# A second gathered list for row tiles 12 to 20 in layer 2 of a four-layer graph kernel

## The chip, the cores and the metric

The kernel runs on one core of one Trainium2 chip. The metric is the device time of one execution in microseconds (us). The kernel before was timed three times: 1455.23, 1458.40 and 1458.63 us, median 1458.4 us. A further execution was recorded by the hardware profiler; it took 1452.67 us, of which the profile's span covers 1450.9 us. All engine times below are from that profiled execution.

## What is computed

There are N = 2708 nodes with 512 features each, and one adjacency matrix `adj` (2708 x 2708). Four layers follow each other, each as a residual step on the normalised features. Layer 2, the one that is changed, is

```python
def _L2_gnn_ref(x, adj, W1, b1, W3, b3, Wf, bf):
    h = jax.nn.relu(adj @ (x @ W1) + b1)
    h = jax.nn.relu(adj @ (h @ W3) + b3)
    return jnp.tanh(h @ Wf + bf)
...
    # --- layer 2 (adj_preln) ---
    h = jnp.maximum(_layernorm(x, axis=-1), 0.0)
    x = x + _L2_gnn_ref(h, adj, L2_gnn_W1, L2_gnn_b1, L2_gnn_W3, L2_gnn_b3, L2_gnn_Wf, L2_gnn_bf)
```

The adjacency is sparse and symmetric in its pattern, and the chance of an edge falls with both node numbers (as one over the square root of each). So a row of low number has many neighbours, and the neighbours of any row crowd towards the low numbers. Layer 3 needs only where `adj` is not zero.

## The kernel before: tiles, stages and order

The rows are cut in 22 tiles of 128 (the last, tile 21, has 20 rows). An aggregation, `adj @ g`, is made for one row tile `m` at a time in `aggregate` (L909 to L970), from two parts:

- **Dense part.** The first `DENSE = 6` column tiles (nodes 0 to 767) are loaded whole, in two pieces of three tiles of 192 KB each (`load_piece`, L881). ACT rounds the piece (`a_hi`, L937), DVE makes the remainder (`a_lo`, L938) and a scaled sum (`a_s`, L939), and TensorE multiplies each column tile three times in the fast format fp32r (L950), into the banks `agg` and `aggs`. That is 18 matmuls per row tile.
- **Listed part.** From node 768 on, only nodes that are a neighbour of some row of the tile are used. Layer 0 has searched them once per row tile into index lists of `CHUNKS[m]` blocks of 128 (6, 6, 6, 5, 6, 5, 5, 5, 5 for tiles 12 to 20). GpSimd fetches the rows of `g` with one indirect DMA per block (`gather`, L901) into one of eight buffers `gg0` to `gg7`, taken in turn (`gathered`, L820). The matching columns of the adjacency lie packed in DRAM from layer 0 and come with one load per row tile (`load_listed`, L892, a ring of two `ac` buffers). TensorE multiplies each block once in full fp32 (L953), into `aggs`.

Row tile 0 has no lists: it multiplies all 22 column tiles whole (L961 to L967).

Layer 2 makes two such passes over the row tiles:

- **First pass** (loop at L1043), order 0 to 9, 21, 10 to 20. Inside tile 0 all 22 tiles of `x @ W1` are also made (`first_product`, L1013): their inputs come through `fetch` into the buffers `slot0` to `slot17`, nine tiles ahead, and each result is stored to the DRAM tensor `g1d`, from which the gathers of tiles 1 to 21 read. Each row tile then goes through bias and relu (`relu_parts`, L838: four transposes into `pt`, L841, then ACT `v_hi` L846, DVE `v_lo` L847 and `v_s` L850) and through twelve matmuls with W3 (`project3`, L866) and is stored to `g2d`. The first pass also notes where `adj` is not zero (`mark`, L919) and stores that per row tile (L969) for layer 3.
- **Second pass** (loop at L1212), order 0, 6 to 9, 21, 10 to 20, 1 to 5. It aggregates from `g2d`, goes through Wf, tanh, the residual, a normalisation and layer 3's W, and stores to `hid`. For its tile 0 the buffers `slot0` on are filled with `g2d`.

Each engine executes its queue in order; SyncE (SP) issues the plain DMAs in order, GpSimd (POOL) the indirect ones. A scheduler in the compiler front end decides how the instructions of neighbouring row tiles are interleaved on each engine, so the order on an engine isn't the order of the program text. In the order as built, TensorE runs the dense matmuls of tile `m + 1` around the transposes and the W3 matmuls of tile `m`, and the listed blocks of tile `m + 1` behind them.

The places that the change and the steps of the prediction touch are these:

- L820: the choice of a gather buffer.
- L892: the load of the packed columns.
- L901 and L953: the gather, and the matmul of a listed block.
- L937 to L950: the split of a dense piece and its matmuls.
- L835: the sum `go`, stored to `g1d` at L1027. The first gather of row tile 1 needs all of `g1d`, the part of node tile 21 included.
- L354, L370, L371 and L377: the way in which layer 0 loads and searches a list. A row of running counts ("ranks") is stored to DRAM by SP, loaded back to all 128 partitions, and DVE looks up where each rank first appears (FIND_INDEX8).
- L320: the running sum on DVE that makes such a row.

Of the kernel before, what the change touches and what calls it, by code (L numbers as in the profile page):

```python
# [9 lines left out]
FP = mybir.dt.float32  # L10
# [12 lines left out]
P = 128  # L23
# [12 lines left out]

DENSE = 6
LEAD = 3
CHUNKS = (0, 10, 9, 8, 7, 7, 7, 7, 6, 6, 6, 6, 6, 6, 6, 5, 6, 5, 5, 5, 5, 2)


@with_exitstack
def kernel(
# [43 lines left out]
    def rows(t):  # L87
        return min(P, N - t * P)
# [37 lines left out]
    BEHIND = DENSE * P  # L126
    WIDE, LOW = (N - BEHIND) // 4, BEHIND // 2
    assert WIDE * 4 == N - BEHIND and WIDE < BLK and LOW * 2 == BEHIND
    cnt_b = dram.tile([NGROUP, P, WIDE], BF, name="cnt_b")
    cnt_l = dram.tile([NGROUP, P, LOW], BF, name="cnt_l")  # L130

# [2 lines left out]

    idx = const.tile([P, NT], U32, name="idx")
    BAD_BOUND, BAD_NEG, BAD_MANY = NT, NT + 1, 2 * NT + 1
    bad = const.tile([P, 3 * NT + 1], FP, name="bad")
    nc.gpsimd.memset(bad, 0.0)
    flag = const.tile([P, 1], I32, name="flag")

# [1 line left out]
    idx_g = const.tile([P, NT, NCH], U32, name="idx_g")  # L142

    rdeg = const.tile([P, NT], FP, name="rdeg")
    ones_b = const.tile([P, 1], BF, name="ones_b")
    nc.gpsimd.memset(ones_b, 1.0)

# [69 lines left out]
    with tc.tile_pool(name="l0_slab", bufs=2) as slabs, tc.tile_pool(  # L217
# [29 lines left out]
        nc.gpsimd.iota(place_i, pattern=[[P, NCH]], base=1, channel_multiplier=1)  # L247
        places = hp.tile([P, NCH], FP, name="places")
        nc.vector.tensor_copy(places, place_i)

        pending, pending_c = [], []

# [551 lines left out]
    NGG = 8  # L804
# [12 lines left out]
    NMARK = DENSE + NCA  # L817
    gather_slot = [0]

    def gathered():  # L820
        name = f"gg{gather_slot[0] % NGG}"
        gather_slot[0] += 1
        return gp.tile([P, D], FP, name=name)

    def sum_banks(dst, main, mixed, n):

# [63 lines left out]
        return raw[:k, : len(ts), :n], k  # L890

    def load_listed(m):  # L892
        ac = ap.tile([P, NCA, P], FP, name="ac")[:, : CHUNKS[m], : rows(m)]
        nc.sync.dma_start(out=ac, in_=listed[m])
        return ac

    def gather(m, gd, gs=None, index=idx_g):

# [10 lines left out]
    def aggregate(m, parts, shifted, gd, marked):  # L909


        n = rows(m)
        whole, num = dense_of(m), CHUNKS[m]
        if marked:
            nz = ap.tile([P, NMARK, P], U8, name="nz", bufs=3)

            def mark(i, a):
                k, ts = a.shape[:2]
                nc.scalar.activation(nz[:k, i : i + ts, :n], a, AF.Sign)  # L919
        main = ps_a.tile([P, D], FP, name="agg") if dense_of(m) else None  # L920
        mixed = ps_a.tile([P, D], FP, name="aggs")
        chunks = []
        if num:
            ac = load_listed(m)
            chunks = [(ac[:, c, :], g) for c, g in enumerate(gather(m, gd))]
            if marked:
                mark(whole, ac)
        for ts in dense if dense_of(m) else []:
            gs = [parts(t) for t in ts]
            raw, k = load_piece(m, ts)  # L930
            hi, lo, s = (
                ap.tile([P, PIECE, P], FR, name=f"a_{part}") for part in ("hi", "lo", "s")
            )
            d = (slice(0, k), slice(0, len(ts)), slice(0, n))
            if marked:
                mark(ts[0], raw)
            nc.scalar.activation(hi[d], raw, AF.Copy, scale=UP)  # L937
            nc.vector.tensor_tensor(lo[d], raw, hi[d].bitcast(FP), ALU.subtract)  # L938
            nc.vector.scalar_tensor_tensor(  # L939
                s[d], lo[d].bitcast(FP), SHIFT, hi[d].bitcast(FP), op0=ALU.mult, op1=ALU.add  # L940
            )
            for i, t in enumerate(ts):
                ghi, glo, gs_ = gs[i]
                first, last = t == 0, t == DENSE - 1
                for acc, a, b, st, sp in (
                    (main, hi, ghi, first, False),
                    (main, lo, glo, False, last),
                    (mixed, s, gs_, first, False),
                ):
                    nc.tensor.matmul(acc[:n], a[:k, i, :n], b[:k], start=st, stop=sp)  # L950
        if chunks:
            for c, (a, g) in enumerate(chunks):
                nc.tensor.matmul(  # L953
                    mixed[:n],
                    a,
                    g,
                    start=(c == 0 and not dense_of(m)),
                    stop=(c == len(chunks) - 1),
                )
        else:  # L960
            for ts in others:  # L961
                gs = [shifted(t) for t in ts]
                raw, k = load_piece(m, ts)
                for i, t in enumerate(ts):
                    nc.tensor.matmul(
                        mixed[:n], raw[:, i, :], gs[i][:k], start=False, stop=(t == NT - 1)
                    )  # L967
        if marked:
            nc.sync.dma_start(out=nonzero[m], in_=nz[:, : whole + num, :n])  # L969
        return main, mixed  # L970
# [69 lines left out]
    w3 = split_w(wsetb, wr, "wb")  # L1040
    wr = load_w(wset, wf_d, "wr")

    for m in order_m:  # L1043
        n = rows(m)
        parts = aggregated(m, first_parts, first_product, g1d, bias1, marked=True)
        if m == 0:
            wf = split_w(wset, wr, "wa")
# [163 lines left out]
    FIRST = 2  # L1211
    for m in order_2:  # L1212
        n = rows(m)
        parts = aggregated(m, second_parts, second_product, g2d, bias3)
        if m == 0:
            w = split_w(wsetb, wr, "wb")
# [499 lines left out]
```

## Time and profile before

| what | us |
|---|---|
| runs before: lowest, median, highest | 1455.23, 1458.40, 1458.63 |
| the profiled execution: its own time, its span | 1452.67, 1450.9 |
| TensorE matmul (PE) busy in the span | 1299.2 (90%) |
| DVE busy | 940.9 (65%) |
| ACT busy | 676.5 (47%) |
| POOL busy | 679.2 (47%) |
| listed blocks, L953: 520 records, two per block | 232.4 |
| dense matmuls, L950: three groups of 252 | 115.4, 102.0, 100.3 |
| gathers of the first pass, L901: 130 | 132.2 |
| gathers of the second pass, L901: 130 | 130.9 |

In the span, row tile 0 of the first pass runs from about 500 to 605 us, the other tiles of that pass from there to about 888 us, the second pass from there to about 1237 us, and layer 3 to the end. Tiles 12 to 20 are the last nine of the first pass (about 776 to 882 us); in the second pass five more tiles follow them.

The mean granted TensorE clock is 0.95; from 605 to 870 us it is 0.99. Busy times of different engines overlap, so the column doesn't add up to the span. A listed block is recorded as two matmuls. Records of consecutive matmuls overlap: a dense matmul has a record of about 0.39 us, and the next one starts 0.23 us later. The difference of start times is what counts on a path.

### The profile page before, as it was taken

Reading aid. Unit: us, or ns where it says so; the run is one execution under the profiler, and the core shown is the slowest. Engines: PE = TensorE matmul, PEld = TensorE weight load, DVE = VectorE, ACT = ScalarE, POOL = GpSimd, SP = SyncE. Lnnn points to the kernel's source line nnn. Section 1 sums busy time; section 2 is a strip of 40 time slices with the busy share of each in tenths; the row PEclk is TensorE's granted clock in tenths of the full one; section 3 lists DMA queues with packets and bytes.
Section 4 is the critical chain, followed back from the end, with each engine's and each line's share of the span. In section 5 each row is a group of like instructions: output and inputs, shape, how many; then the busy total and the mean of one; then the engine's idle time right before and its main releaser. Section 6 shows DMA issues by size and latency. Waiting matters only on the chain. (4 is left out here: it accounts for less than half of the span.)

```text
span 1450.9 us, 15435 instructions
## 1 busy us (share of the span) xinstructions
PE 1299.2 (90%) x4400; PEld 767.0 (53%) x4400; DVE 940.9 (65%) x1907; ACT 676.5 (47%) x1040; POOL 679.2 (47%) x690
## 2 busy tenths in 40 slices
PE   6489988999987489899999998999999999778997
PEld 2134433444433266556656665666767666556664
DVE  2579988989898588533343445565666666565674
ACT  5998637454111365422233334444455445454443
POOL 1174567777655311265444432343333435257762
PEclk9699999999998699999999999999999999888998
DMA  8999999998893885488777777656556666378884
GB/s 301 305 384 307 318 322 334 338 276 273 285 339 108 282 268 182 154 256 266 237 217 236 232 242 255 179 187 193 164 164 188 196 195 204 122 251 264 257 260 145
DMA packets 195940, 351.27 MB, mean 242 GB/s; under 512 B 26444, under 2 KB 107692, under 8 KB 192113
## 3 DMA queue, kind: packets, MB, share of 16 engines
q1 hardware_dynamic: 148453, 200.68, 41.3%
q0 software_dynamic: 47392, 149.51, 32.6%
q8 instruction: 37, 0.61, 0.2%
q14 instruction: 58, 0.48, 0.1%
HBM read 286.99 MB, written 63.12 MB: 241 GB/s over the span
## 5 line engine op out<-in xcount | busy, mean ns | idle before, releaser
L953 PE MATMUL aggs<-gg,ac 128*128 128x512 f32 (+1 forms) x520 | 232.4, 594 | 4.6 <-DMA gg<-g1d,idx_g 4.6
L901 POOL DMA_INDIRECT gg<-g2d,idx_g x130 | 130.9, 1007 | 218.6 <-PE aggs L953 169.4
L901 POOL DMA_INDIRECT gg<-g1d,idx_g x130 | 132.2, 1017 | 175.5 <-PE aggs L953 105.1
L532 POOL DMA_INDIRECT ac<-in_adj_t_dram,idx_a x130 | 140.4, 1080 | 83.4 <-issue 33.2
L745 PE MATMUL acc<-h,inc 128*128 128x512 f32 x348 | 165.2, 616 | 14.3 <-DVE inc L600 11.4
L953 PEld LDWEIGHTS aggs<-gg,ac 128*128 128x128 f32 (+1 forms) x520 | 97.4, 188 | 111.3 <-issue 101.2
L550 POOL DMA_INDIRECT h<-h0d,idx_g x111 | 114.9, 1035 | 52.7 <-issue 24.1
L950 PE MATMUL agg<-ghi,a_hi 128*128 128x512 f32 x252 | 115.4, 458 | 3.5 <-ACT a_hi L937 3.3
L937 ACT ACTIVATE a_hi<-raw 128x384 fp32r<-128x384 f32 x84 | 43.5, 520 | 159.3 <-issue 86.9
L745 PEld LDWEIGHTS acc<-h,inc 128*128 128x128 f32 x348 | 64.9, 196 | 91.6 <-issue 68.9
L950 PE MATMUL agg<-glo,a_lo 128*128 128x512 f32 x252 | 102.0, 405 | 2.5 <-ACT glo L200 2.5
L745 PE MATMUL acc<-h,incl 128*128 128x512 f32 (+1 forms) x222 | 103.7, 615 | 0.0
L950 PE MATMUL aggs<-gs,a_s 128*128 128x512 f32 x252 | 100.3, 401 | 0.1
L901 POOL DMA_INDIRECT gg<-hidr,idx_h x79 | 78.0, 988 | 46.2 <-PE agg L1137 15.2
L938 DVE TENSOR_TENSOR a_lo<-raw,a_hi 128x384 fp32r<-128x384 f32 x84 | 47.3, 563 | 78.7 <-ACT a_hi L937 53.6
L157 PE MATMUL yacc<-wvo,hT 128*128 128x512 f32 (+1 forms) x176 | 87.3, 642 | 9.8 <-ACT hT L186 9.8
L847 DVE SCALAR_TENSOR_TENSOR v_lo<-pt,v_hi 128x512 fp32r<-128x512 f32 (+1 forms) x88 | 56.7, 665 | 45.5 <-ACT v_hi L846 45.0
L828 DVE SCALAR_TENSOR_TENSOR u<-aggs,u 128x512 f32<-128x512 f32 x42 | 28.9, 687 | 76.2 <-PE aggs L953 74.6
L745 PEld LDWEIGHTS acc<-h,incl 128*128 128x128 f32 (+1 forms) x222 | 43.2, 197 | 54.2 <-issue 49.8
L846 ACT ACTIVATE v_hi<-pt 128x512 fp32r<-128x512 f32 (+1 forms) x88 | 48.6, 578 | 43.3 <-PE pt L841 41.3
L483 ACT ACTIVATE sgn<-ar 128x2708 bf16<-128x2708 f32 (+1 forms) x22 | 54.0, 2455 | 28.6 <-DMA ar<-in_adj_dram 28.2
L514 DVE FIND_INDEX8 at_top<-top,ar 128x8 uint32<-128x2708 f32 (+1 forms) x22 | 65.3, 2970 | 0.0
(276 smaller groups left out, 2768.1 us busy)
## 6 DMA issues: line engine op xcount, KB each, us to landing
ar<-in_adj_dram SPq DMA_DIRECT2D x27, 1354.0 KB
raw<-in_adj_t_dram SPq DMA_DIRECT2D x108, 192.0 KB
slot<-x SPq DMA_DIRECT2D x41, 256.0 KB
at<-in_adj_t_dram SPq DMA_DIRECT2D x27, 384.0 KB
ranks<-rank_b SPq DMA_DIRECT2D x20, 485.0 KB
ac<-lst SPq DMA_DIRECT2D x16, 384.0 KB
h<-in_x_dram SPq DMA_DIRECT2D x21, 256.0 KB
h0d<-h POOLq DMA_DIRECT2D x21, 256.0 KB, 7.0
```

The lines of the kernel that those rows point to most:

```text
L157: nc.tensor.matmul(acc[:n], hT[:, c, :n], w[:, c, :], start=(c == 0), stop=(c == NCD - 1))
L483: nc.scalar.activation(sgn[:n], ar[:n], AF.Sign, accum_out=sum_sgn[:n])
L514: nc.vector.max_index(at_top[:n], top[:n], ar[:n])
L532: nc.gpsimd.indirect_dma_start(out=ac[:, c, :n], out_offset=None, in_=adj_units, in_offset=bass.IndirectOffsetOnAxis(ap=idx_a[:, m, c0 + c ...
L550: nc.gpsimd.indirect_dma_start(out=g, out_offset=None, in_=h0d[:, :], in_offset=bass.IndirectOffsetOnAxis(ap=idx_g[:, m, c : c + 1], axis=0),)
L745: nc.tensor.matmul(acc[:n], a, g, start=(i == 0), stop=(i == len(pairs) - 1))
L846: nc.scalar.activation(hi[d], pt[d], AF.Relu, scale=UP)
L847: nc.vector.scalar_tensor_tensor(lo[d], pt[d], 0.0, hi[d].bitcast(FP), op0=ALU.max, op1=ALU.subtract)
L901: nc.gpsimd.indirect_dma_start(out=gs[c], out_offset=None, in_=gd[:, :], in_offset=bass.IndirectOffsetOnAxis(ap=index[:, m, c : c + 1], ax ...
L938: nc.vector.tensor_tensor(lo[d], raw, hi[d].bitcast(FP), ALU.subtract)
L950: nc.tensor.matmul(acc[:n], a[:k, i, :n], b[:k], start=st, stop=sp)
L953: nc.tensor.matmul(mixed[:n], a, g, start=(c == 0 and not dense_of(m)), stop=(c == len(chunks) - 1),)
```

## The change

For row tiles 12 to 20 only the first two column tiles are still multiplied whole (6 matmuls instead of 18). The nodes between them and the old lists, 256 to 767, go into a second list of two blocks per row tile, of which both the rows of `g` and the columns of the adjacency are gathered by GpSimd, in each pass anew. In this case's data the lists have 184 to 239 entries for their 256 places. A list that doesn't fit sets a flag (`bad`), which makes the kernel take a slower, general path at the end.

The lists are made in layer 2 itself. `few_ranks` takes layer 0's counts for rows 12 to 20 from DRAM, makes the running sums (DVE) and stores them to `rank_f`. `load_few_ranks` loads the row of one tile to all partitions (128 KB) into `slot7` to `slot15`, buffers that held inputs of `x @ W1` before. `few_search` makes the list of one tile with some ten small DVE instructions. In the program text these stand two row tiles apart and five to seven row tiles ahead of their use. In the order as built, the nine loads and nine searches stand close together, around the end of row tile 0 of the first pass.

For the tiles with second lists, `slot1` to `slot4` serve as four further gather buffers (not for tiles 18 to 20 of the first pass, when those slots are being filled with `g2d`). In the first pass both dense pieces are still loaded, and marked for layer 3; in the second pass only the piece's first two column tiles are.

```diff
+SPARSE, FEW, FEW_CHUNKS = 12, 2, 2
...
+    more_places = [[]]
+
     def gathered():
-        name = f"gg{gather_slot[0] % NGG}"
+        names = [f"gg{i}" for i in range(NGG)] + more_places[0]
+        name = names[gather_slot[0] % len(names)]
...
+    def few_ranks():
+        r = NFULL - SPARSE
+        total, rank = (
+            gp.tile([P, D], FP, name=f"slot{i}").bitcast(to) for i, to in ((5, BF), (6, HF))
+        )
+        for g in range(r // GROUP):
+            nc.sync.dma_start(
...
+        rank = rank[:r, :BETWEEN]
+        nc.vector.tensor_scalar_min(rank, total[:r, FEW * P : DENSE * P], 1.0)
+        nc.vector.tensor_tensor_scan(rank, rank, rank, 0.0, ALU.add, ALU.max)
+        nc.sync.dma_start(out=rank_f[SPARSE:NFULL], in_=rank)
+
+    def load_few_ranks(m):
+        few[m] = gp.tile([P, D], FP, name=f"slot{7 + m - SPARSE}").bitcast(HF)
+        nc.sync.dma_start(
+            out=few[m][:, :BETWEEN], in_=rank_f[m : m + 1].to_broadcast([P, BETWEEN])
+        )
+
+    def few_search(m):
...
+        nc.vector.tensor_scalar_add(end, ranks[:, BETWEEN - 1 : BETWEEN], 1.0)
+        nc.vector.tensor_copy(ranks[:, BETWEEN:], end)
+        nc.vector.tensor_scalar(want, places_f, end, None, op0=ALU.min)
+        nc.vector.max_index(at, want, ranks)
...
+    def gather_few(m, gd, ac):
+        gs = [gathered() for _ in range(FEW_CHUNKS)]
+        for dst, src, i in [(ac[:, c, :], adj_units, FEW_A + c) for c in range(FEW_CHUNKS)] + [
+            (g, gd[:, :], FEW_G + c) for c, g in enumerate(gs)
+        ]:
+            nc.gpsimd.indirect_dma_start(
...
+        return [(ac[:, c, :], g) for c, g in enumerate(gs)]
...
         if num:
-            ac = load_listed(m)
+            ac, ac_few = load_listed(m)
             chunks = [(ac[:, c, :], g) for c, g in enumerate(gather(m, gd))]
             if marked:
                 mark(whole, ac)
-        for ts in dense if dense_of(m) else []:
+        taken = whole
+        if is_sparse(m):
+            taken = FEW
+            chunks += gather_few(m, gd, ac_few)
+        for ts in dense if whole else []:
+            if not marked:
+                ts = [t for t in ts if t < taken]
+                if not ts:
+                    continue
+            raw, k = load_piece(m, ts)
+            if marked:
+                mark(ts[0], raw)
+            ts = [t for t in ts if t < taken]
+            if not ts:
+                continue
+            raw = raw[:, : len(ts)]
             gs = [parts(t) for t in ts]
-            raw, k = load_piece(m, ts)
...
-    for m in order_m:
+    for i, m in enumerate(order_m):
         n = rows(m)
+
+        more_places[0] = [f"slot{i}" for i in range(1, 5)] if SPARSE <= m < NFULL - 3 else []
+        if m == SPARSE // 2 - 4:
+            few_ranks()
+        if is_sparse(m + SPARSE // 2 + 1):
+            load_few_ranks(m + SPARSE // 2 + 1)
+        if is_sparse(m + SPARSE // 2 - 1):
+            few_search(m + SPARSE // 2 - 1)
         parts = aggregated(m, first_parts, first_product, g1d, bias1, marked=True)
...
     for m in order_2:
         n = rows(m)
+        more_places[0] = [f"slot{i}" for i in range(1, 5)] if is_sparse(m) else []
         parts = aggregated(m, second_parts, second_product, g2d, bias3)
```

## The prediction, made before the changed kernel had run

> **What bounds the kernel now.** I read the page's table of engines first, then busy time by stage, then the waits of the first pass behind its tile 0, and last PE's instructions of one row tile.
>
> ```profile
> PE 1299.2 (90%) x4400; PEld 767.0 (53%) x4400; DVE 940.9 (65%) x1907; ACT 676.5 (47%) x1040; POOL 679.2 (47%) x690
> ```
>
> PE is busiest, but 90% is a mean over stages. By stage (PE, PEld, DVE, ACT, POOL busy, then clock, DMA share, GB/s):
>
> ```profile
> 750.00:800.00 50.00, 49.81 (x179) 30.90 (x178) 21.69 (x37) 15.70 (x29) 24.36 (x24) 1.00 0.73 231
> 800.00:870.00 70.00, 69.71 (x252) 43.94 (x251) 29.98 (x50) 23.68 (x45) 28.76 (x29) 1.00 0.73 236
> 1100.00:1140.00 40.00, 39.97 (x156) 27.24 (x156) 26.52 (x50) 20.51 (x32) 16.46 (x16) 1.00 0.61 188
> ```
>
> Where the changed row tiles run, in both passes, PE is full: 69.71 of 70, at full clock. POOL has half its time free, the DMA engines a quarter.
>
> ```profile
> POOL gg L901 <- PE aggs L953: 105.1, 46, 8.9
> POOL gg L901 <- DMA nz<-nz: 45.1, 1, 45.1
> PE aggs L953 <- DMA gg<-g1d,idx_g: 4.6, 2, 3.3
> ```
>
> From 605 to 870 us POOL waits for PE to free gather buffers (105.1 us); PE waits for gathers only 4.6. The single 45.1 is POOL's wait through tile 0: the first gather starts at 605.90, after the last part of g1d, whose sum is this one:
>
> ```profile
> 602.66 0.67 DVE L835 TENSOR_TENSOR go<-aggs,go 20x512 f32<-20x512 f32 x1
> ```
>
> One row tile on PE (start, duration):
>
> ```profile
> 751.13 0.39 PE L950 MATMUL aggs<-gs,a_s 128*128 128x512 f32 x1
> 751.36 5.31 PE L953 MATMUL aggs<-gg,ac 128*128 128x512 f32 x12
> 756.10 0.79 PE L950 MATMUL agg<-ghi,a_hi 128*128 128x512 f32 x1
> 756.73 0.40 PE L950 MATMUL agg<-glo,a_lo 128*128 128x512 f32 x1
> ...
> 764.26 5.31 PE L953 MATMUL aggs<-gg,ac 128*128 128x512 f32 x12
> ```
>
> A dense matmul takes 0.23 us from start to start. Six listed blocks take 756.73 - 751.36 - 0.23 = 5.14, so 0.857 each. The period is 764.26 - 751.36 = 12.90 us, of which 18 x 0.23 = 4.1 is dense, 5.1 listed, 0.7 the four transposes, 2.93 W3 (759.73 to 762.66).
>
> **What the Trainium skill says.** "DMA: Bandwidth & Descriptors", section "SWDGE vs HWDGE vs iDMA": DMAs of GpSimd and of SyncE feed different queues of the same engines, which take turns. The page's two queues agree: 41.3% and 32.6% of the same 16 engines. So added gathers slow plain loads too. The same page, "Anatomy of one DMA — SWDGE (gpsimd) path", prices a DMA at about 2.0 us plus bytes over 436 GB/s, 2.6 us for a gather of 256 KB; the trace shows a median of 4.8 to landing at 770 to 870 us and 6.8 for layer 0's h gathers at 180 to 260 us, so I use the trace. "VectorE: DVE Perf Modes", section "The TRN2 errata — SBUF-src ops pay a fixed extra latency per instruction": tiny operations aren't free. The trace agrees: 0.142 us for one 128x1 addition (L370).
>
> **First pass, tiles 12 to 20.** Removed: 12 dense matmuls, 12 x 0.231 = 2.77 us. Added: two blocks, 1.71. Net -1.06 per tile, x 9 = -9.5. New periods: 11.85 (six old blocks), 11.0 (five). The splits on ACT and DVE shrink by two thirds; both have over half their time free here, so I cost them at nothing, as I do the dropped piece.
>
> Is POOL late then? A gather starts 1.25 us after the one before (0.95 and 0.30). A tile needs old blocks + 4: ten or nine, 12.5 or 11.25 us, 0.25 to 0.65 more than PE's period. Over nine tiles POOL falls behind by about 4 us. It has a lead: twelve buffers instead of eight for tiles 12 to 17, and its order puts four gathers of tiles 12 and 13 into an early gap, 5 us of work. I replayed both queues by hand with these prices: tile 20's blocks end at 872.1 instead of 881.2, so -9.1.
>
> The DMA engines are tighter. The nine tiles move about 234 GB/s x 105.3 us = 24.6 MB. Added per tile: two gathers of 256 KB and two of 64 KB, 0.655 MB; together 30.5 MB in 96 us, 317 GB/s. At 180 to 260 us the engines carried 329 GB/s at a share of 0.97. So it just fits; landings go towards 6.8 us and some gathers will be late. I allow 1.6 us: -7.5. Bounds: -9.5 (all hidden) and 0 (DMA full).
>
> **Second pass, the same tiles.** The same -9.5 on PE; a 64 KB tile x 4 less is loaded, DMA has room (0.61). But a chain loses cover: from the end of the Wf product to the normalised row (sum, bias, tanh, residual, norm: 1065.7 to 1073.4, 7.7 us) PE now covers with dense matmuls and listed blocks, 8.8 us (1065.6 to 1074.48). Afterwards it has 6 x 0.23 + 8 x 0.857 = 8.2 us for six-block tiles and 7.4 for five-block tiles. With semaphores I take 7.9 for the chain; in the order built the short cover meets about five tiles, x 0.6 = 3.0: -6.5. Bounds: -9.5, and -3.5 if every tile loses 0.65.
>
> **The new lists, at the end of tile 0.** DVE gains the minimum and running sum, 0.65 (as a 128x512 operation, 0.69) + 1.29 (L320: 1.22 for 485 elements, to 512) = 1.9 us, and nine searches: eight small operations at 0.14, 0.08 for MATCH_VALUE_LOAD, FIND_INDEX8 at 2.17 x 513/1941 = 0.57, so about 1.7 us, 15 us in all. SP gains three count loads, one store and nine loads. Text spreads these over tiles 2 to 15; the built order pulls them forward. On DVE the running sum stands before the sum at 571.65, two searches behind the one at 576.39, four more up to the sum of g1d's last tile (602.66), the others behind it.
>
> DVE is idle about 14 us from 571 to 603, but it executes in order. Step one: the rank row is stored at 573.7; layer 0 issues a load 3.2 us after such a store (54.1 to 57.3), so 576.9; landing isn't shown for 128 KB: at least 2.3 by the page's price, at most 6.9 (485 KB: issued 57.3, used 64.2); I take 4.0, so 580.9. Two searches, then the split v_lo that PE needs at 581.82 is done at about 585: PE, which was idle under 1 us here, stands 3.2. Step two: the load into slot12 waits for PE's transposes of tile 21 (597.68 + 0.42 + 3.2), lands 4 us later at 605.3; half its search (1.2) and two weight splits (1.29) stand ahead of the last sum: 607.8 instead of 602.66. Behind it wait the g1d store on SP and all gathers of tile 1. So +5.1; with 0.3 for the early gathers +5.3. Bounds: +2 (quick landings), +9 (6.9 each, and one more wait). SP's queue behind these loads holds g1d stores and raw pieces of tile 1: same wait, not a second.
>
> The g2d loads of slot1 to slot4 move behind tile 17's blocks, needed only in the second pass: nothing.
>
> **Sum.** -7.5 - 6.5 + 5.3 = -8.7. On the profiled 1452.67 us (span 1450.9) that is 1444. The median of the three runs is 5.7 above the profiled one: 1458.4 - 8.7, rounded up, 1450. A difference under about 0.3% (4.4 us) can't be told from no change by this measurement.
>
> **Rivals.**
> - A, the transfers take PE's place in the first pass: 317 GB/s proves too much or POOL's lead is spent early, and it gives -1.5 there. -1.5 - 6.5 + 5.3 = -2.7: 1455.7. For it: DMA share near 0.98, nine POOL gathers over PE's period. Against: 329 GB/s was carried, and the lead.
> - B, everything is hidden: -9.5 - 9.5 + 0.5 = -18.5: 1440. For it: DVE's 14 idle us, loads landing fast. Against: the order of DVE, and the chain's 7.7 us against a cover of 7.4.
> - C, slower: the searches ahead of g1d's last sum don't find idle time, since each waits in order for its own load while PE waits for DVE's splits. Price: 15.3 + 1.9 + 7.2 (3.2 and 4.0) = 24.4 us, against 14 saved: +10.4, 1469. It decides as soon as the front costs more than 14 us. Against: three of the nine searches stand behind the last sum.
> - That the second lists don't fit and the general path runs: excluded, the data uses 184 to 239 of 256 places.
>
> **Chances.** Forecast 0.47 (own range 1445 to 1455), A 0.18, B 0.15, C 0.20. Faster by over 0.3% (below 1454.0): 0.43 of the forecast, all of B, 0.05 of A: 0.63. Slower: C but for 0.02, and 0.01 of A: 0.19. Within: the remaining 0.18. The range leaves out the faster half of B and the upper half of C: 1441 to 1463.
>
> **What would show it.** Right: PE periods near 11.9 and 11.0 us for tiles 12 to 20 of the first pass, 14.1 to 14.9 in the second; first gather of tile 1 near 611; DMA share above 0.9 there. Wrong: PE waiting long for gathers (A), first gather still near 606 (B) or past 620 (C). Should a search take much more than 1.7 us, or the scheduler's order meet loads that land late, the front is wrong; should landings pass 7 us, the first pass.

## The result, and the profile after

The changed kernel is slower: 1463.59 us median of 8 runs (1454.56 to 1469.06), against 1457.82 us for 8 runs of the kernel before; ratio 1.0055, 95% interval 1.0031 to 1.0080. The forecast was 1450 with a range of 1441 to 1463. It failed in its sign.

The profiled execution of the changed kernel took 1469.06 us (span 1467.3), the slowest of its eight; the profiled one of before, 1452.67, was near the fast end of its own. So the two traces differ by 16.4 us of span where the medians differ by 5.8, and some stages differ from run to run. This table splits the 16.4 by events that both traces have. Its last column says what the forecast gave.

| stage (from event to event) | before | after | difference | forecast |
|---|---|---|---|---|
| to the first store of g1d | 506.6 | 512.0 | +5.4 | 0 |
| first to last store of g1d (tile 0 of the first pass) | 96.8 | 97.6 | +0.8 | +5.3 with the row below |
| to the sum `go` of row tile 11 | 172.6 | 176.7 | +4.1 | |
| sum of tile 11 to sum of tile 20 (tiles 12 to 20) | 110.9 | 115.5 | +4.6 | -7.5 |
| to the tanh of tile 0, second pass | 34.1 | 36.0 | +1.9 | 0 |
| to the tanh of tile 11 | 116.5 | 114.6 | -1.9 | -6.5 with the two below |
| to the tanh of tile 20 | 145.4 | 144.7 | -0.7 | |
| to the last tanh (tile 5) | 85.3 | 87.5 | +2.2 | |
| layer 3, to the end of the span | 182.7 | 182.7 | 0 | 0 |

The first row lies before the change takes effect. That event fell at 502.8 to 516.5 us in the traces of sixteen kernels measured on chips of about this speed, so I don't count it. The row of tile 11 also moves with the run (170.4 to 181 in those traces); here PE ran at a mean clock of 0.96 from 615 to 750 us instead of 0.99, and waited 3.0 us for a gather. What stays is the row of tiles 12 to 20: a loss in place of a gain.

The page's first line, and the stretch from 800 to 870 us, in the profile after (us; PE, PEld, DVE, ACT, POOL busy; clock, DMA share, GB/s):

```profile
PE 1291.9 (88%) x4256; PEld 744.8 (51%) x4256; DVE 933.9 (64%) x1964; ACT 664.5 (45%) x1022; POOL 745.8 (51%) x762
```

```profile
800.00:870.00 70.00, 57.54 (x178) 33.31 (x177) 24.52 (x41) 20.88 (x42) 41.48 (x44) 0.93 0.79 254
```

PE had 7 us less to do and was idle for 12.5 us of the stretch 800 to 870, where before it was idle for 0.3. The DMA share is 0.79 here; 0.92 was carried in a run below, so the transfers aren't full. POOL was busy 41.5 of the 70 us.

The waits of the profile after, from 770 to 890 us (total, times, longest):

```profile
DVE go L920 <- ACT go L919: 46.5, 8, 9.4
ACT nz L1018 <- DMA ac<-lst: 42.1, 8, 8.8
```

Before, ACT waited 14.6 us for the packed columns in this stretch, never longer than 2.4. Now it waits up to 8.8 us at a time. The order of ACT's queue shows what stands behind that wait (profile after, ACT):

```profile
814.30 0.74 ACT L1018 ACTIVATE nz<-ac 128x640 uint8<-128x640 f32 x1 [8.04 <-DMA ac<-lst]
814.94 0.92 ACT L1018 ACTIVATE nz<-raw 128x384 uint8<-128x384 f32 x2
815.77 0.57 ACT L919 ACTIVATE go<-main 128x512 f32<-128x512 f32 x1
...
827.61 0.84 ACT L1018 ACTIVATE nz<-ac 128x768 uint8<-128x768 f32 x1 [7.75 <-DMA ac<-lst]
```

ACT marks the packed columns of a later tile ahead of the sum `go` of this one. And here is why the columns are late (profile after, SP's queue, start of each issue):

```profile
815.49 1.01 SPq L969 DMA_DIRECT2D raw<-in_adj_t_dram  x2
817.10 0.34 SPq L1171 DMA_DIRECT2D g2d<-go  x1
823.77 0.34 SPq L1182 DMA_DIRECT2D slot<-g2d  x1
824.21 0.37 SPq L979 DMA_DIRECT2D ac<-lst  x1
```

The same tile (13) before:

```profile
802.67 0.32 SPq L1052 DMA_DIRECT2D g2d<-go  x1
805.56 0.38 SPq L884 DMA_DIRECT2D raw<-in_adj_t_dram  x1
806.00 0.48 SPq L1063 DMA_DIRECT2D slot<-g2d  x1
808.33 0.32 SPq L894 DMA_DIRECT2D ac<-lst  x1
```

SP's waits for the landing of that store, from 770 to 890 us, before and then after (total, times, longest):

```profile
SPq L1063 <- DMA g2d<-go: 4.2, 5, 2.8
SPq L1182 <- DMA g2d<-go: 34.1, 8, 6.7
```

SP's order of these three was already this one before: store `g2d`, load it back into `slot` for the second pass (which waits for the store's landing, the arrival of its bytes), then the next packed load. One thing differs: before, a raw piece is loaded between the store and the slot load, and after, two raw pieces go directly ahead of the store. So there is a ring, a loop in which each step waits for the one before: packed load lands, 3.5 us after its issue at 810.80; mark and sum, 1.5; to the store, 1.3; the slot load waits for its landing, 6.7; the packed load, 0.4. That is 13.4 us. Sums follow each other at 815.8, 829.2 and 843.8, 13.4 and 14.6 us apart: the first is this ring's time, and neither is PE's 11 to 12 us. Before, the store took 2.0 to 3.7 us to let the slot load go, and PE's 12 to 13 us per tile hid the ring.

A second hold-up stands once, at 845 us (profile after; SP, then ACT, then PE):

```profile
845.63 3.54 SPq L1182 DMA_DIRECT2D slot<-g2d  x4
```

```profile
853.11 1.28 ACT L196 ACTIVATE ghi<-slot 128x512 fp32r<-128x512 f32 x2 [7.96 <-DMA slot<-g2d]
854.30 0.58 ACT L931 ACTIVATE v_hi<-pt 128x512 fp32r<-128x512 f32 x1
```

```profile
854.93 2.08 PE L951 MATMUL main<-wb,v_hi 128*128 128x512 f32 x4 [6.88 <-ACT v_hi L931]
```

These are the loads of slot1 to slot4, which the change uses as gather buffers until tile 17. ACT's split of them for the second pass stands in its queue in the middle of the first pass, ahead of `v_hi`; PE stood 6.9 us behind it, and came back with half its speed (2.08 us for four matmuls that took 1.12 before).

In the second pass one tile of the profile after looks like this (PE):

```profile
1107.64 1.04 PE L926 MATMUL pt<-ident,u 128*128 128x128 f32 x8
1108.92 1.21 PE L951 MATMUL main<-wb,v_hi 128*128 128x512 f32 x4 [0.25 <-ACT v_hi L931]
...
1113.73 1.09 PE L951 MATMUL mixed<-wa,v_s 128*128 128x512 f32 x4
1115.13 0.50 PE L1061 MATMUL agg<-ghi,a_hi 128*128 128x512 f32 x1 [0.30 <-ACT u L912]
...
1122.86 1.04 PE L926 MATMUL pt<-ident,u 128*128 128x128 f32 x8
```

In the profile before, the same places look like this:

```profile
1106.49 1.04 PE L841 MATMUL pt<-ident,u 128*128 128x128 f32 x8
1107.29 0.48 PE L950 MATMUL aggs<-gs,a_s 128*128 128x512 f32 x1
1107.78 1.19 PE L866 MATMUL main<-wb,v_hi 128*128 128x512 f32 x4
...
1112.73 1.10 PE L866 MATMUL mixed<-wa,v_s 128*128 128x512 f32 x4
1113.67 0.39 PE L950 MATMUL agg<-glo,a_lo 128*128 128x512 f32 x1
```

The period after is 15.2 us (1107.64 to 1122.86), with seven listed blocks and six dense matmuls. Before, a period with six blocks and 18 dense matmuls took 15.98 (1074.5 to 1090.5); less one block, 0.857, that makes 15.1 for a tile with five: PE lost 1.06 us of work and no time in this tile. The page still calls PE busy. The steps between groups tell more. From the transposes to the product behind them it is 1.3 us in both, but before a dense matmul ran inside that step. From the last product to the first dense matmul it is now 1.40 us, before 0.94. At 0.23 us a dense or product matmul and 0.857 a block, a period had 1.2 us beyond these before and has 2.3 in this stretch.

Over the whole pass the traces do show a gain, and its loss. From the tanh of tile 0 to that of tile 20 it takes 259.1 to 259.4 us in each of twelve traces with lists in this pass, and 261.9 to 262.1 in each of four without: 2.7 us less, of 6.5 forecast. But the last stretch, tiles 1 to 5, which have no second lists, takes 86.3 us on average with them and 83.7 without. Why was not looked into.

### The profile page after: what moved, and what is told of

It is laid out like the page before. It is cut to its first block, busy times and chain, and to the rows that moved or that the text cites. A ratio compares the mean times of both kernels' runs of the same rounds, so it can differ in the third digit from the quotient of the medians.

```text
span 1467.3 us, 15346 instructions
## 1 busy us (share of the span) xinstructions
PE 1291.9 (88%) x4256; PEld 744.8 (51%) x4256; DVE 933.9 (64%) x1964; ACT 664.5 (45%) x1022; POOL 745.8 (51%) x762
## 5 line engine op out<-in xcount | busy, mean ns | idle before, releaser
L1064 PE MATMUL aggs<-gg,ac 128*128 128x512 f32 (+1 forms) x514 | 236.7, 599 | 6.8 <-DMA gg<-g1d,idx_g 6.8
L1000 POOL DMA_INDIRECT gg<-g1d,idx_g x119 | 119.5, 1004 | 137.5 <-PE aggs L1064 63.7
L1000 POOL DMA_INDIRECT gg<-g2d,idx_g x111 | 107.9, 972 | 146.7 <-PE aggs L1064 105.7
L1000 POOL DMA_INDIRECT gg<-hidr,idx_h x79 | 78.2, 990 | 46.7 <-PE agg L1256 13.3
L1048 ACT ACTIVATE a_hi<-raw 128x384 fp32r<-128x384 f32 (+1 forms) x66 | 32.3, 491 | 139.2 <-issue 66.0
L1061 PE MATMUL agg<-ghi,a_hi 128*128 128x512 f32 x180 | 85.9, 477 | 5.4 <-ACT a_hi L1048 3.3
L920 DVE TENSOR_TENSOR go<-mixed,go 128x512 f32<-128x512 f32 (+1 forms) x33 | 22.7, 689 | 82.0 <-ACT go L919 69.4
L1061 PE MATMUL agg<-glo,a_lo 128*128 128x512 f32 x180 | 73.4, 408 | 0.1
L1061 PE MATMUL aggs<-gs,a_s 128*128 128x512 f32 x180 | 71.8, 408 | 0.0
L1049 DVE TENSOR_TENSOR a_lo<-raw,a_hi 128x384 fp32r<-128x384 f32 (+1 forms) x66 | 34.4, 521 | 58.0 <-ACT a_hi L1048 35.0
```

Source lines behind the costliest of these rows:

```text
L1000: nc.gpsimd.indirect_dma_start(out=gs[c], out_offset=None, in_=gd[:, :], in_offset=bass.IndirectOffsetOnAxis(ap=index[:, m, c : c + 1], ax ...
L1064: nc.tensor.matmul(mixed[:n], a, g, start=(c == 0 and not dense_of(m)), stop=(c == len(chunks) - 1),)
```

## The experiments

All ratios are to the kernel before on the same chip, with a 95% interval. The chips of the first four groups ran the kernel before in 1454.6 to 1455.2 us; the last one in 1508. "Tail" is the time from the sum of tile 11 to the sum of tile 20 in the profiled execution, 110.9 in the kernel before. Theory 1 is the one of the queues, as above; theory 2, its rival, puts the loss down to the transfers or to GpSimd.

| run | ratio | interval | tail, us |
|---|---|---|---|
| changed kernel | 1.0055 | 1.0031 to 1.0080 | 115.5 |
| first pass only | 1.0039 | 1.0021 to 1.0056 | 114.2 |
| second pass only | 0.9983 | 0.9963 to 1.0003 | 112.2 |
| lists unused | 0.9980 | 0.9957 to 1.0002 | 110.6 |
| eight buffers | 1.0055 | 1.0031 to 1.0078 | 111.0 |
| packed load by GpSimd | 1.0096 | 1.0066 to 1.0126 | 114.8 |
| eight buffers, packed load by GpSimd | 1.0008 | 0.9993 to 1.0023 | 106.5 |
| no matrix gathers | 1.0034 | 1.0014 to 1.0055 | 115.8 |
| before, packed load by GpSimd | 0.9995 | 0.9972 to 1.0018 | 109.2 |
| late marks | 1.0085 | 1.0059 to 1.0111 | 115.4 |
| eight buffers, late marks | 1.0048 | 1.0031 to 1.0065 | 112.6 |
| second pass only, dense matmuls twice | 0.9988 | 0.9971 to 1.0005 | 112.1 |
| from tile 15, eight buffers, late marks | 1.0060 | 1.0036 to 1.0085 | 119.3 |
| eight buffers, packed load by ACT | 0.9989 | 0.9970 to 1.0008 | 105.6 |
| eight buffers, slots from g1d | 0.9995 | 0.9971 to 1.0019 | 104.4 |
| slots from g1d | 1.0021 | 1.0004 to 1.0038 | 107.9 |
| eight buffers, slots from g1d, no matrix gathers | 0.9943 | 0.9925 to 0.9962 | 98.4 |
| columns early | 1.0113 | 1.0060 to 1.0165 | 97.9 |
| columns early, first pass only | 1.0063 | 1.0039 to 1.0087 | 100.2 |

**First pass only.**

```diff
-        if is_sparse(m):
+        if is_sparse(m) and marked:
             taken = FEW
...
-        more_places[0] = [f"slot{i}" for i in range(1, 5)] if is_sparse(m) else []
+        more_places[0] = []
```

> Second lists in the first pass only; the second pass keeps its 18 dense matmuls and eight gather buffers. Theory 1 (queues: the first pass loses its gain to loads that come late in SP's queue and hold up ACT, the second pass does gain some 3.5 us): this is 3 to 4 us slower than the changed kernel, some 9 us slower than before. Theory 2 (transfers: the added gathers cost time wherever they run, in the second pass too): this is faster than the changed kernel.

Measured: 1.0039, tail 114.2. Slower than before, but not slower than the changed kernel (1.0055, the intervals overlap). Neither theory's number is hit. The loss comes from the first pass: with lists there the kernel is slower, and the next run, without, isn't.

**Second pass only.**

```diff
-        if is_sparse(m):
+        if is_sparse(m) and not marked:
             taken = FEW
...
-        more_places[0] = [f"slot{i}" for i in range(1, 5)] if SPARSE <= m < NFULL - 3 else []
+        more_places[0] = []
```

> Second lists in the second pass only; the first pass is as before but for the making of the lists. Theory 1: the end of tile 0 costs 6 us, the second pass gives back 3.5, so 2 to 3 us slower than before, and no stall of PE over 1 us from 750 to 890 us. Theory 2: 6 us slower than before or more, since the second pass gains nothing.

Measured: 0.9983, not to be told from before. No stall over 1 us from 750 to 890 us, as theory 1 said; but the 6 us at the end of tile 0 aren't there.

**Lists unused.**

```diff
-        if is_sparse(m):
+        if False:
             taken = FEW
```

and both `more_places` empty.

> The lists are made, but no pass uses them: rank rows, loads and searches alone. Theory 1: the searches ahead of the sum of the last part of g1d delay the first gather by about 6 us, and the kernel with it: 6 us slower than before. Rival (DVE's idle time takes the searches, and the 6 us seen in the trace come from the granted clock): within 2 us of before.

Measured: 0.9980. My theory's 6 us fall: making the lists costs nothing that can be measured. On this the rival is right (2.9 us below before, where it said within 2, but the interval takes in no change). Of the 6 us by which the first gather was late in the trace after, 5.4 were there before tile 0 began (the first row of the table); that the clock made them isn't shown. The three runs also add up: (1.0039 - 0.9980) for the use in the first pass, (0.9983 - 0.9980) for the use in the second, -0.0020 for the lists, together 1.0042 against 1.0055. In us of 1455 the first pass costs 8.6 (give or take 4.1), and the second gives nothing that shows (0.4, give or take 4.4).

**Eight buffers.**

```diff
-        more_places[0] = [f"slot{i}" for i in range(1, 5)] if SPARSE <= m < NFULL - 3 else []
+        more_places[0] = []
```

(in the first pass)

> The changed kernel, but with the eight old gather buffers in the first pass, so that slot1 to slot4 are filled with g2d as early as before. Theory 1: ACT's split of those slots no longer waits for them (8 us of waiting, 6.9 us of PE in the trace): 5 to 8 us faster than the changed kernel. Theory 2: the gathers have less lead, PE waits for them instead: as slow as the changed kernel, or slower.

Measured: 1.0055, no gain in the time; the tail is 111.0 instead of 115.5, and no PE wait for `v_hi` over 1 us is left in it. So the late slots explain 4.5 us of the trace's tail, but the runs don't show the gain, whose size is about that of their interval. Nor is the tail the whole loss: here it is as long as in the kernel before, and the kernel is still 0.55% slower. ACT's wait for packed columns is still 50.8 us here, up to 9.0 at a time.

**Packed load by GpSimd**, with twelve buffers, with eight, and in the kernel before.

```diff
-        nc.sync.dma_start(out=ac[:, : CHUNKS[m]], in_=listed[m])
+        eng = nc.gpsimd if marked else nc.sync
+        eng.dma_start(out=ac[:, : CHUNKS[m]], in_=listed[m])
```

> The changed kernel, with the load of the packed columns issued by GpSimd instead of SyncE in the first pass. Theory 1 (in SP's queue this load stands behind the load of slot from g2d, which waits for the landing of the g2d store of the same tile; ACT's mark of the packed columns waits for it, and ACT's sum for the next g2d store stands behind the mark, so each tile takes one round of this ring, about 14 us): the periods of tiles 13 to 16 fall below 12 us, 4 to 6 us faster than the changed kernel, ACT's wait of 8 us for late slots stays. Theory 2 (the DMA engines are full, landings are long whoever issues): no gain, GpSimd's added issue makes it 1 to 3 us slower.

> As the run before it, and with the eight old gather buffers in the first pass. Theory 1: both hold-ups are gone, tiles 12 to 20 of the first pass take 102 to 104 us instead of 111 from the sum of tile 11 to that of tile 20, and the kernel is 7 to 9 us faster than with eight places alone, a little faster than before. Theory 2: 109 us or more, and no gain.

> The kernel before, with the load of the packed columns issued by GpSimd in the first pass: the control for the two runs above. Both theories: PE is full there and waits for no packed columns, within 2 us of before.

Measured: 1.0096, 1.0008, 0.9995. With eight buffers the tail falls to 106.5; with twelve PE stands 10.4 us behind ACT's wait for the slots and all is lost. The expectation of 102 to 104 is missed too, and the trace of the run with eight buffers shows why. POOL's queue there:

```profile
843.82 1.36 POOL L989 DMA_INDIRECT gg<-g1d,idx_g  x1 [0.30 <-issue]
845.18 0.59 POOL L980 DMA_DIRECT2D ac<-lst  x1
846.08 0.97 POOL L1001 DMA_INDIRECT gg<-g1d,idx_g  x1 [0.30 <-issue]
847.35 0.94 POOL L989 DMA_INDIRECT ac<-in_adj_t_dram,idx_g  x1 [0.30 <-issue]
```

From 800 to 860 us POOL has nothing but its 0.3 us between issues: it is the bound, with ten or nine gathers and a load per tile. The packed load waits its turn behind gathers instead of behind a store.

**No matrix gathers.**

```diff
-        for dst, src, i in [(ac[:, c, :], adj_units, FEW_A + c) for c in range(FEW_CHUNKS)] + [
-            (g, gd[:, :], FEW_G + c) for c, g in enumerate(gs)
-        ]:
+        for dst, src, i in [(g, gd[:, :], FEW_G + c) for c, g in enumerate(gs)]:
```

> The changed kernel without the two gathers of adjacency columns per tile and pass; the two blocks are multiplied by the first two packed columns instead, so this part of the aggregation is left out. GpSimd issues 36 gathers less, the DMA engines move 2.4 MB less. Theory 1: the ring through SP's queue is untouched, within 2 us of the changed kernel in the first pass. Theory 2: GpSimd and the transfers have room again, 4 us faster or more, mostly in the first pass.

Measured: 1.0034, tail 115.8. With 36 gathers less the tail is as long as ever: theory 2 isn't the first bound. The slot load still goes 5.8 to 7.0 us after the store there (DMA share 0.77 from 790 to 850 us), so the longer landing doesn't come from these gathers. The two raw loads issued directly ahead of the store would fit, but that was not tried alone. The ratio, 3.1 us below the changed kernel's, lies within the intervals.

**Late marks**, with twelve buffers, with eight, and with eight from tile 15 on.

```diff
-            if marked:
-                mark(whole, ac)
...
-        if marked:
-            nc.sync.dma_start(out=nonzero[m], in_=nz[:, : whole + num, :n])
+        def rest():
+            if num:
+                mark(whole, ac)
+            nc.sync.dma_start(out=nonzero[m], in_=nz[:, : whole + num, :n])
+        if marked:
+            late_marks.append(rest)
...
         nc.sync.dma_start(out=g2d[span(m)], in_=go[:n])
+        late_marks.pop()()
```

> The changed kernel; the mark of the packed columns, and the store of the marks, follow the g2d store of their own row tile in the program text, so that ACT no longer waits for the packed columns of a later tile ahead of its sum go. Theory 1b (it is ACT's order that closes the ring, not who issues the load): no wait of ACT for packed columns over 3 us in tiles 13 to 16, their periods 11 to 12 us; the wait for late slots stays (7 to 10 us of PE). 4 to 6 us faster than the changed kernel. Rival (GpSimd's ten gathers per tile, 12.5 us, bound the tail): no gain.

> As the run before it, with the eight old gather buffers in the first pass. Theory 1b: both hold-ups are gone, 102 to 105 us from the sum of tile 11 to that of tile 20 (111 before), 3 to 6 us faster than the kernel before. Rival (GpSimd): 106 us or more, since eight buffers give it no lead; level with the kernel before.

> As eight buffers with late marks, with second lists from row tile 15 on instead of 12 (24 gathers less per pair of passes, six tiles instead of nine). If the lists pay per tile, the gain shrinks to two thirds: 2 to 4 us faster than before. If GpSimd is the bound, tiles with five old blocks fare better than those with six and this equals or beats the list from 12 on.

Measured: 1.0085, 1.0048, 1.0060. Missed. In all three the scheduler still puts a mark ahead of the sum, ACT still waits for packed columns (54.0 us from 770 to 890 with eight buffers, 11.6 at most), and PE has a new stall behind `v_hi`, of 3.5 and 3.3 us near 762 us in the first two and of 5.7 near 800 in the third. These runs changed an order without opening the ring, and tell nothing for or against it. They did move the raw loads: they stand behind the store here, and with twelve buffers the slot load follows the store of tiles 11 to 14 by 2.7 to 5.0 us instead of the changed kernel's 6.1 to 7.1. With eight buffers the two ranges overlap (4.3 to 5.2 and 4.3 to 6.1), so the raw loads are at most a part of the long landing. The one from tile 15 has its tail spread over other tiles, and I draw nothing from it.

**Dense matmuls twice**, in the second pass alone.

```diff
+                    reps = 2 if is_sparse(m) and not marked else 1
+                    for again in range(reps):
```

> Second lists in the second pass only, with each of the six dense matmuls of tiles 12 to 20 issued twice there (the first two column tiles are counted twice in the aggregation). PE has 6 x 0.231 x 9 = 12.5 us more to do in the second pass. If the second pass gains little because PE stands idle between dependent steps for want of dense matmuls to run meanwhile, part of that is hidden: 4 to 8 us slower than second lists in the second pass alone. If PE is busy throughout, all 12 us show.

Measured: 0.9988 against 0.9983 for the second pass only, 0.7 us (give or take 3.8) for 12.5 us of PE work. From the tanh of tile 11 to the last one the traces take 233.1 against 230.5, all of it behind the tanh of tile 20 (to there 142.5 against 144.7). So PE's work isn't what the second pass waits for. One tile of this run (PE):

```profile
1105.58 1.04 PE L926 MATMUL pt<-ident,u 128*128 128x128 f32 x8
1106.38 0.48 PE L1063 MATMUL agg<-glo,a_lo 128*128 128x512 f32 x1
1106.87 1.19 PE L951 MATMUL main<-wb,v_hi 128*128 128x512 f32 x4
...
1111.79 1.10 PE L951 MATMUL mixed<-wa,v_s 128*128 128x512 f32 x4
1112.73 0.63 PE L1063 MATMUL aggs<-gs,a_s 128*128 128x512 f32 x2
```

A dense matmul stands again between the transposes and the product, and the step from the last product to the next matmul is 0.94 instead of 1.40. A period has 1.2 us beyond its matmuls again, as before. The added work fills the gaps that its removal had opened.

**Packed load by ACT**, eight buffers.

```diff
-        nc.sync.dma_start(out=ac[:, : CHUNKS[m]], in_=listed[m])
+        eng = nc.scalar if marked else nc.sync
+        eng.dma_start(out=ac[:, : CHUNKS[m]], in_=listed[m])
```

> The changed kernel with eight gather buffers in the first pass, and the load of the packed columns issued by ACT there. Ring theory: the load no longer stands behind the g2d store and the slot load in SP's queue, so ACT's mark finds it early: 102 to 106 us from the sum of tile 11 to that of tile 20 (eight buffers alone: 111), 4 to 7 us faster than eight buffers alone. Rival (GpSimd or the landings bound the tail): 109 us or more.

Measured: 0.9989, tail 105.6. The tail is as the ring theory said; the gain, 0.0066 less than eight buffers alone, is 9.6 us of 1455 (give or take 4.4), above the 4 to 7 forecast. ACT's waits for packed columns from 770 to 890 us fall from 50.8 to 11.7. The landings are no shorter: SP's slot load still follows the store by 4.9 to 6.9 us for tiles 11 to 17. It holds up nothing now, since the packed load no longer stands behind it.

**Slots from g1d**, with eight buffers, with twelve, and with eight and no matrix gathers.

```diff
-            nc.sync.dma_start(out=g2[t][:n], in_=g2d[span(t)])
+            nc.sync.dma_start(out=g2[t][:n], in_=g1d[span(t)])
```

> Eight gather buffers in the first pass, and the slots for tile 0 of the second pass are loaded from g1d, which is long complete, instead of g2d (so the second pass computes from other data in its whole matmuls). Nothing in SP's queue waits for the landing of a g2d store any more; bytes and numbers of transfers stay. Ring theory: the ring shrinks from about 14 to 8 or 9 us, below PE's 11: 102 to 106 us from tile 11 to tile 20. Rival: 109 us or more, the bytes are the same.

> As the run before it with the twelve buffers of the changed kernel. Ring theory: tiles 13 to 16 at 11 to 12 us each, but PE still stands 6 to 10 us where ACT waits for slot1 to slot4, whose buffers come free late: 108 to 112 us from tile 11 to tile 20. If the late slots were late only through the g2d stores: 102 to 106 us.

> Eight buffers, slots from g1d, and without the two gathers of adjacency columns per tile and pass (the blocks take the first two packed columns instead). If GpSimd's rate is the next bound behind the ring, its eight or seven gathers now fit under PE: 2 us or more faster than with those gathers, 101 to 103 us from tile 11 to tile 20. If not, within 1 us of that run.

Measured: 0.9995, 1.0021 and 0.9943; tails 104.4, 107.9 and 98.4. This is the cleanest test. The first of them moves the same bytes in the same number of transfers, only SP no longer waits for a store (its queue):

```profile
823.13 0.34 SPq L1171 DMA_DIRECT2D g2d<-go  x1
826.27 0.34 SPq L979 DMA_DIRECT2D ac<-lst  x1
```

The packed load follows the store by 2.8 to 5.0 us for tiles 11 to 17, with eight buffers alone by 4.8 to 6.7; ACT's waits for packed columns fall from 50.8 us to 13.3, the tail from 111.0 to 104.4, and the time by 0.0060 (8.7 us, give or take 4.9). With twelve buffers the tail is 3.5 us longer, with a PE stall of 5.8 us behind `v_hi`: in the trace the late slots are a cause of their own. The times of this pair lie within their intervals (0.0026), those of the pair with GpSimd's packed load don't (1.0096 against 1.0008). Without matrix gathers the tail is 6.0 us shorter and the time 0.0052: GpSimd's rate was the next bound. That it wasn't the transfers shows in the stretch 790 to 850 us, with the gathers and then without:

```profile
790.00:850.00 60.00, 57.13 (x187) 32.40 (x185) 21.56 (x35) 18.31 (x35) 45.71 (x47) 1.00 0.89 279
790.00:850.00 60.00, 60.00 (x201) 35.50 (x200) 22.74 (x38) 20.00 (x39) 39.72 (x40) 1.00 0.90 285
```

The DMA share is the same, and PE is full. With the gathers POOL issues 47 in 60 us, which at 1.25 us each fills it. At 98.4 the tail beats what I forecast for it (110.9 - 9.1 = 101.8).

**Columns early.** A version meant to beat both: eight buffers, packed load by ACT, and the adjacency columns gathered once in GpSimd's idle time in tile 0, stored to DRAM and loaded with the packed columns.

```diff
+    def pack_few(m):
+        cols = gp.tile([P, D], FP, name=f"slot{7 + m - SPARSE}")[:, : FEW_CHUNKS * P].rearrange(
+            "p (c k) -> p c k", c=FEW_CHUNKS
+        )
+        for c in range(FEW_CHUNKS):
+            nc.gpsimd.indirect_dma_start(
...
+        nc.sync.dma_start(out=few_cols[m], in_=cols)
```

> A version meant to beat both kernels: eight gather buffers in the first pass, the packed load issued by ACT there, and the adjacency columns of the second lists gathered once, early, while GpSimd is idle, stored to DRAM and loaded with the packed columns in both passes. GpSimd then has eight or seven gathers per tile, 10.0 or 8.8 us against PE's 11.9 or 11.0. Ring and GpSimd theories: 98 to 102 us from the sum of tile 11 to that of tile 20 and 5 to 8 us faster than before (ratio 0.994 to 0.997). What could undo it: the stores of the columns stand in SP's queue ahead of the last g1d store.

> The same with the second lists in the first pass only. If the second pass gains nothing from them because PE's work is not what it waits for, this is within 3 us of the run before it; if they do pay there, it is 3 to 6 us slower.

Measured: 1.0113 and 1.0063. The tail is what was asked for (97.9 and 100.2), and yet both are slower than before. Both traces lose time around row tile 1 (ACT's queue, columns early):

```profile
674.73 0.52 ACT L1066 ACTIVATE a_hi<-raw 128x384 fp32r<-128x384 f32 x1 [21.88 <-remote]
683.10 0.60 ACT L948 ACTIVATE v_hi<-pt 128x512 fp32r<-128x512 f32 x1 [7.85 <-remote]
```

PE had finished the transposes that `v_hi` reads by 671.7 us, and stood 10.4 us for `v_hi`; in the other run it is 10.4 us as well. ACT comes to `v_hi` late, and the profile doesn't name what held it (its "remote" is a release that it can't place). Whether the program does this or the chip, which ran all kernels some 50 us slower, is open. In the second pass, too, the two runs differ: from the tanh of tile 11 to that of tile 20 it takes 152.8 us with the lists and 145.5 without, where the other chips showed 144.7 and 145.5. So the forecast that lists in the second pass are worth nothing met a loss here, and its cause is open too. What these two runs do show is the tail: against the run with ACT's packed load and eight buffers (105.6) the columns' bytes still move, as loads of ACT, and only GpSimd's issues are gone from it.

## Why the prediction was wrong

- **PE full, POOL half free, DMA three quarters.** Read rightly. The conclusion, that PE's work was the price of a tile, was not: it held only so long as PE was the longest of several loops, and one of 13.4 us came to stand above PE's 11 to 12.
- **First pass, -7.5: this is the step that failed.** Measured about +8.6 us. What it left out is ACT's wait for the packed columns, 14.6 us before and 42.1 after, with the sum standing behind it. PE's saving is real: between the two sums PE had 104 dense matmuls less and 15 blocks more, 11.0 us, and where the hold-ups were taken away the tail took 98.4 and 97.9 us, 12.5 and 13 less than before. Three things took its place, in this order. The ring through SP's queue (opened by the slots from g1d: 111.0 to 104.4, with 0.0060 of the kernel's time; by ACT's issue: to 105.6, with 0.0066). The late slots, 3.5 to 4.5 us in traces. GpSimd's rate, 6.0. The tail isn't all: the times of the thirteen kernels of about 1455 us with lists in the first pass lie 0 to 10 us, 4.8 on average, above what their tails alone would give. From the sum of tile 20 to the first tanh they take 36.1 us on average, the five without 34.3; where the rest lies isn't known.
- **"The g2d loads of slot1 to slot4 ... needed only in the second pass: nothing."** Wrong. Their results are, but ACT's splits of them stand ahead of `v_hi` in the first pass, and PE stood 6.9 us. I named the DMA queue that the loads moved in and not the engine that reads them.
- **The splits and marks on ACT at nothing.** I looked at ACT's busy share. ACT was free and yet late, because the mark ahead of its sum waited for a load. I never followed who waits for a packed load that comes late.
- **POOL.** My replay gave it a lead enough for -9.1. The bound was there, but behind the ring: with eight buffers and the ring opened 104.4, against 101.8.
- **DMA.** The allowance of 1.6 us was for landings that get long because the engines fill. The share reached 0.79 to 0.85, not 0.98, and PE was full at 0.90 with the slots from g1d and no matrix gathers. That added gathers slow plain loads was not shown by any run. A landing did get long (2 to 3.7 us before, up to 7.1 after, for the g2d store as SP sees it), and it decided because a queue waited on it.
- **Second pass, -6.5.** Measured nothing (0.9983 against 0.9980). The mechanism, lost cover, was named, and its size was wrong: I priced one long chain (7.4 against 7.9 us, a gap of 0.5 that the sum took as 0.6), and what was lost was short covers of 0.25 to 0.5 us between dependent groups, 1.1 us per tile in the stretch shown. That left 2.7 us at the tanh of tile 20, and nothing at the end of the pass. Doubling the dense matmuls cost 0.7 us of 12.5.
- **The end of tile 0, +5.3.** Measured 0.8 in the trace and no loss in the runs. The work was as priced (1.75 us for the first search, 1.7 forecast). The waits weren't: the rank row's load was issued 2.2 us after its store (3.2 forecast), and the first search started 3.1 us later without waiting (4.0); the last of the searches ahead of g1d's last sum waited 0.16 us. DVE's idle time took the rest: rival B was right on this step. The least landing, 2.3 us, used the price of GpSimd's path, and this was a load of SyncE. The sign named for this step, a first gather near 611, did come (612.2), but by luck: 5.4 us of it were there before tile 0 began.
- **Rivals.** C ended on the right side with 1469, but for a cause that isn't there. A named transfers and GpSimd's rate: the second is a part of it. The ring wasn't among the rivals.

What the Trainium skill says in "DMA: Bandwidth & Descriptors", section "Anatomy of one DMA — SWDGE (gpsimd) path", that most of the fixed cost of a DMA is the receipt of the last write, bears on the ring: SP waited 2.0 us at least, and up to 7.1, between a 256 KB store and the load that reads it. It is a statement on GpSimd's path; that it holds for SyncE's store no run here separates.

Open: what lengthens the landing of the store; where the loss outside the tail lies, and why tiles 1 to 5 of the second pass get longer; why twelve buffers with GpSimd's packed load, and with late marks, lost more than the changed kernel; what held ACT and the second pass in the runs with early columns. No version was found that beats the kernel before beyond the interval with its outputs kept: of those with lists in the first pass the nearest, ACT's packed load with eight buffers (0.9989), is level with it, as is the second pass only (0.9983).

## What to carry to other kernels

Before pricing work that you take from a full engine, follow each load that this stage issues around its ring: who waits for it, what stands behind that wait, and which store or buffer lets the next load go; the longest ring, not the busy share, is what the stage falls back to. Where you give buffers a second use, look for every instruction that reads their next content, and for what stands behind it in its queue. Matmuls that stand between dependent steps are cover: here, taking them out was worth little, since nothing else came to stand there.

## What the runs showed of the hardware that was not expected

- PE came back slow from a long stall: after 6.9 us of waiting, four matmuls took 2.08 us instead of 1.12, and the granted clock of 800 to 870 us was 0.93, against 1.00 with no stall.
- The wait of SP between the g2d store and the load behind it went from 2.0 to 3.7 us to 6.1 to 7.1 us for tiles 11 to 14, and was 5.8 to 7.0 us without the matrix gathers, at a DMA share of 0.77 as well as at 0.85.
- GpSimd started gathers 1.25 us apart when it had nothing to wait for. With ten or nine per tile that bound a stage at a DMA share of 0.89; with eight or seven, PE was full at a share of 0.90.
- Runs of the kernel before spread over 12 to 28 us on one chip (1447.75 to 1462.49 on one of them), and one chip ran it in 1508; only ratios on one chip tell a change of half a per cent.
